# Attention kernel on one Trainium2 core: layer 0 scores in groups of up to seven PSUM banks, and results of three chunks written for the next layer

**The chip, the cores and the metric.** One NeuronCore of one Trainium2 chip. The time is the device time of the kernel in microseconds (us), median of several executions. The executions of one round share a chip; the rounds of the experiments ran on chips 12, 15 and 9, each with the kernel before beside them.

## The reference, cut to what matters

```python
# x: (8, 64, 64, 64) float32, so b=8, c=64, n=4096; c8=8
def layer0(x):                      # 8-channel attention over the pixels
    f = Wf @ x + bf;  g = Wg @ x + bg;  hh = Wh @ x + bh     # (8,n) (8,n) (64,n)
    beta = softmax(einsum('bci,bcj->bij', f, g), axis=2)     # 4096 x 4096 per batch
    return x + einsum('bcj,bij->bci', hh, beta)

def layer1(x):                      # group norm, 64-channel attention, projection
    q, k, v = split(w_qkv @ group_norm(x) + b_qkv)
    attn = softmax(q.T @ k * 64**-0.5)
    return w_proj @ (attn @ v) + b_proj + x

out = layer1(layer0(x))
```

## The kernel before

There are 16 stages: layer 0 of batches 0 and 1, layer 1 of batch 0, then layer 0 and layer 1 in turn, with layer 1 of batch 7 last. A stage has four chunks of 512 queries for each half of the pixels, and each chunk 16 steps over the keys. A layer 0 step makes four score banks (two blocks `p` by two halves `h`), each by one matmul on a 32x128 tile. ScalarE turns them into exponentials, TensorE weighs the values with them on 128x64 tiles, and VectorE adds them up for the softmax's denominator.

The kernel uses eight PSUM banks of 512 columns: three tiles of two banks for scores and products, and two for accumulators.

```python
ps_s = ctx.enter_context(tc.tile_pool(name="ps_s", bufs=3, space=PSUM))   # 3 x 2 banks
ps_a = ctx.enter_context(tc.tile_pool(name="ps_a", bufs=2, space=PSUM))   # 2 x 1 bank
# ...
for i, (at, c) in enumerate(seq):               # every chunk c of every stage
    j = 0
    while j < 2 * NT:                           # 32 blocks of two banks
        due, taken = take(i * NT + (j + at.group) // 2 - 1)   # inserted work of this step
        blocks = range(j, min(j + (2 if taken else at.group), 2 * NT))  # at.group: 3 in layer 0
        group = []
        for j in blocks:                        # scores of this group
            t, p = divmod(j, 2)
            ps = ps_s.tile([P, 2, CW], F32, tag="s", name=...)
            at.scores(ps, t, p, c)
            group.append((j, ps))
        for j, ps in group:                     # one exp of 1024 columns per block
            # ... a new tile e for every second block
            nc.scalar.activation(e[:, p], ps, AF.Exp, scale=at.scale)
        for u in due: u[2]()                    # inserted products, results
        for r in ready: weigh(*r, now)          # weighing of the group BEFORE
        ready = new
```

`take` hands out inserted work that was put down for a step: the projections of the next stage (`fg`, `qk`), its values (`v`), the denominators (`z`), and a chunk's result. Values are a product whose PSUM bank is emptied by a copy on VectorE:

```python
def values(self, src, w, c):
    ps = ps_s.tile([P, 2, CW], F32, tag="s", name=...)
    # ... 32 small matmuls
    self.copy_values(self.vt[...], ps[...])     # copy_values = nc.vector.tensor_copy
```

A finished chunk's result is a chain on VectorE: `reciprocals` (add, reciprocal, then two DMAs that spread it), and `result` (multiply, add to x, statistics of the next layer's norm):

```python
at_step(now + delay, lambda: sums(spare), not spare)
at_step(now + delay + wait, reciprocals, False)
at_step(now + delay + 2 * wait, result, False)
```

## Time and profile before

| | before |
|---|---|
| median time (3 runs) | 3134.6 us |
| TensorE / VectorE / ScalarE busy | 98 / 80 / 66% |
| layer 0 of batches 0 and 1 | 166.8 and 165.2 us |
| layer 0 of batches 2 to 7 | 151.5 us each |
| layer 1 stages | about 233 us each, the last 241 |

A stage here lasts from its first exp to the first exp of the next. The prediction shows the main views. Timelines there have start, duration, engine, line, operation, output <- input, with the idle time before it and its cause in brackets. The columns are engine, what it was to write, what it waited for, then us in total, times, longest.

```profile
PEld s_l L123 <- ACT e_l L659: 54.1, 69, 0.8
...
PE s_l L123 <- ACT e_l L659: 5.2, 13, 0.4
...
PEld s_l L123 <- DVE v_l L282: 2.0, 3, 1.2
...
PE s_l L123 <- DVE v_l L282: 1.1, 2, 0.8
```

Matmuls (the PE rows) wait for exps for 5.2 us, and for value copies (`DVE v_l`) twice, 1.1 us in all. Weight loads wait for copies for 2.0 us; they run ahead of matmuls, so that does not count by itself. The timeline around one such copy (start, duration, engine, line, operation, output <- input, with the idle time before it and its cause in brackets):

```profile
269.18 0.69 PE L123 MATMUL v_l<-wvp,xn_l 64*64 64x64 f32 x32
269.81 1.94 PE L123 MATMUL acc_l<-e_l,v_l 128*64 128x512 f32 x8
...
271.17 0.68 DVE L282 COPY v_l<-v_l 128x512 f32<-128x512 f32 x1
```

The product is over when the next weighing starts, at 269.81, and its copy starts at 271.17, 1.4 us later.

### The profile page before, as it was taken

The numbers are of one execution on the slowest core, as the hardware profiler recorded it, in microseconds if no ns is written. First come the engines' busy times: TensorE is split into PE (matmuls) and PEld (weight loads), VectorE is DVE, ScalarE is ACT, GpSimd is POOL, SyncE is SP. The second block draws the span as 40 slices with busy tenths as digits, with TensorE's granted clock in tenths as the row PEclk, the third lists the DMA queues.
The fourth block names the chain that finished last, engine by engine and source line by source line (L and its number), as shares of the span: only waits on it lengthen the run. The fifth ranks groups of instructions, "written<-read, shape, count | busy, mean of one in ns | idle before, by whom it ended". The sixth has DMA issues, their size and how long they took to land.

```text
span 3133.8 us, 58576 instructions
## 1 busy us (share of the span) xinstructions
PE 3082.4 (98%) x25523; PEld 1145.6 (37%) x25523; DVE 2505.2 (80%) x1624; ACT 2061.3 (66%) x2224; POOL 16.5 (1%) x41
## 2 busy tenths in 40 slices
PE   7999999999999999999999999999999999999998
PEld 2333334433343334433344333343333433333433
DVE  6999777798768987689776897778977699676676
ACT  5787655786557865578655785558855588555554
POOL 2000000000000000000000000000000000000000
PEclk9999999999999999999999999999999999999999
DMA  3000110100101001010010100101001000000000
GB/s 83 21 8 18 25 25 15 31 8 22 25 17 29 8 22 25 18 28 8 22 25 19 28 8 21 30 13 30 10 18 35 8 18 8 5 21 15 12 11 12
DMA packets 61817, 63.15 MB, mean 20 GB/s; under 512 B 34944, under 2 KB 35024, under 8 KB 61552
## 3 DMA queue, kind: packets, MB, share of 16 engines
q1 hardware_dynamic: 60432, 59.16, 7.7%
q8 instruction: 202, 3.31, 0.4%
q14 instruction: 63, 0.52, 0.1%
q0 software_dynamic: 800, 0.15, 0.0%
q10 hardware_dynamic: 320, 0.01, 0.0%
HBM read 25.06 MB, written 8.65 MB: 11 GB/s over the span
## 4 chain that ended last, share of the span: by engine, by line
PE 86%; DVE 6%; ACT 3%; issue 2%; DMA 2%; SPq 1%; ACTq 0%; DVEq 0%
PE acc_l L123 50%; PE s_l L123 32%; DVE esum_l L625 5%; ACT e_l L659 3%; PE z_l L123 1%; PE qk_l L123 1%; PE v_l L123 1%; DMA r_l<-recips 1%; SPq L320 1%; DMA zt_l<-zs_l 0%; PE fg_l L123 0%; DMA recips<-stash 0%; SPq L412 0%; DVE raw_l L344 0%; DMA w<-in_WgT_dram 0%
## 5 line engine op out<-in xcount | busy, mean ns | idle before, releaser
L659 ACT ACTIVATE e_l<-s_l 128x1024 f32<-128x1024 f32 x2048 | 1968.7, 1025 | 1030.9 <-PE s_l L123 1030.6
L625 DVE TENSOR_TENSOR esum_l<-esum_l,e_l 128x2048 f32<-128x2048 f32 x896 | 2050.8, 2289 | 388.6 <-ACT e_l L659 346.8
L123 PE MATMUL acc_l<-e_l,v_l 64*64 64x512 f32 (+1 forms) x8704 | 1106.2, 591 | 0.0
L123 PE MATMUL s_l<-kq_l 64*64 64x512 f32 (+1 forms) x8448 | 1019.5, 586 | 5.7 <-ACT e_l L659 3.3
L123 PE MATMUL acc_l<-e_l,vt_l 128*64 128x512 f32 x3584 | 841.2, 603 | 0.7
L123 PEld LDWEIGHTS acc_l<-e_l,v_l 64*64 64x64 f32 (+1 forms) x8704 | 382.3, 133 | 549.8 <-issue 504.4
L123 PEld LDWEIGHTS s_l<-kq_l 64*64 64x64 f32 (+1 forms) x8448 | 372.0, 134 | 571.3 <-issue 520.3
L123 PEld LDWEIGHTS acc_l<-e_l,vt_l 128*64 128x64 f32 x3584 | 230.5, 137 | 457.7 <-issue 446.8
L123 PE MATMUL s_l<-fg_l 32*128 32x512 f32 x1792 | 230.3, 468 | 14.6 <-ACT e_l L659 8.2
L123 PEld LDWEIGHTS s_l<-fg_l 32*128 32x128 f32 x1792 | 92.2, 183 | 276.4 <-ACT e_l L659 188.5
L625 DVE TENSOR_TENSOR esum_l<-e_l,e_l 128x2048 f32<-128x2048 f32 x64 | 146.2, 2285 | 27.7 <-ACT e_l L659 27.7
L344 DVE TENSOR_TENSOR raw_l<-raw_l,r_l 128x512 f32<-128x512 f32 x64 | 44.1, 689 | 80.0 <-DMA r_l<-recips 79.9
L123 PE MATMUL z_l<-esum_l,ones 128*32 128x512 f32 (+2 forms) x508 | 55.9, 504 | 4.1 <-DVE esum_l L296 2.8
L551 DVE COPY raw_l<-acc_l 128x512 f32<-128x512 f32 x32 | 22.1, 692 | 36.6 <-PE acc_l L123 36.6
L327 DVE RECIPROCAL stash<-zt_l 128x8 f32<-128x8 f32 x63 | 12.7, 202 | 42.4 <-DMA zt_l<-zs_l 41.4
L525 ACT ACTIVATE kq_l<-qk_l,qkb 128x512 f32<-128x512 f32 x64 | 40.7, 696 | 1.3 <-PE qk_l L123 1.3
L296 DVE TENSOR_TENSOR esum_l<-esum_l 128x1024 f32<-128x1024 f32 x32 | 38.9, 1215 | 0.0
L123 PE MATMUL qk_l<-xn_l,wqk 64*64 64x512 f32 x256 | 33.9, 592 | 2.1 <-ACT e_l L659 2.1
L315 ACT COPY zs_l<-z_l 128x512 f32<-128x512 f32 (+1 forms) x63 | 31.1, 494 | 0.2 <-PE z_l L123 0.2
L282 DVE COPY v_l<-v_l 128x512 f32<-128x512 f32 x36 | 24.7, 686 | 6.9 <-PE v_l L123 6.9
L123 PEld LDWEIGHTS v_l<-wh,x 64*64 64x64 f32 x1024 | 22.4, 135 | 15.4 <-issue 13.3
L123 PEld LDWEIGHTS v_l<-wvp,xn_l 64*64 64x64 f32 x1024 | 21.5, 134 | 16.0 <-issue 14.6
(87 smaller groups left out, 360.5 us busy)
## 6 DMA issues: line engine op xcount, KB each, us to landing
r_l<-recips SPq DMA_DIRECT2D x126, 128.0 KB, 2.9
fg_l<-high_l SPq DMA_DIRECT2D x224, 64.0 KB, 2.0
x<-in_x_dram SPq DMA_DIRECT2D x32, 256.0 KB, 4.9
kq_l<-kq_l SPq DMA_DIRECT2D x64, 128.0 KB, 2.3
out_dram<-raw_l SPq DMA_DIRECT2D x64, 128.0 KB, 2.4
kq_l<-high_l SPq DMA_DIRECT2D x32, 64.0 KB, 2.0
zt_l<-zs_l SPq DMA_DIRECT2D x128, 2.0 KB, 1.8
zt_l<-zs_l SPq DMA_DIRECT2D x124, 1.0 KB, 1.7
```

What stands on the lines that cost most here:

```text
L123: in_order(nc.tensor.matmul(*args, **kwargs))
L282: self.copy_values(self.vt[:, :, ts(c, TPC), :], ps[:, :, 0 : TPC * C].rearrange("k p (t c) -> k p t c", c=C),)
L296: nc.vector.tensor_add(esum[:, 0], esum[:, 0], esum[:, 1])
L315: nc.scalar.copy(zs, z[:, 0:width])
L320: nc.sync.dma_start(dst, zs[row : row + 1, :])
L327: nc.vector.reciprocal(rt, zh)
L344: nc.vector.tensor_mul(raw, raw, r)
L525: nc.scalar.activation(self.parts[:, h, cols], ps[:, h, :], AF.Identity, bias=k1["qkb"][:, h : h + 1],)
L551: nc.vector.tensor_copy(raw, acc[0])
L625: nc.vector.tensor_add(esum, first if t == 1 else esum, e)
L659: nc.scalar.activation(e[:, p], ps, AF.Exp, scale=at.scale)
```

## The change

The intent: fewer, larger groups in layer 0, so that TensorE switches between its two tile shapes less often and ScalarE needs fewer instructions; and less VectorE work inside layer 0, by putting results of its first three chunks into layer 1, where VectorE has room.

```diff
-    ps_s = ctx.enter_context(tc.tile_pool(name="ps_s", bufs=3, space=PSUM))
-    ps_a = ctx.enter_context(tc.tile_pool(name="ps_a", bufs=2, space=PSUM))
+    psum = ctx.enter_context(tc.tile_pool(name="psum", bufs=1, space=PSUM))
+    banks = psum.tile([P, 8, CW], F32, name="banks")
+    pairs = [banks[:, 2 * k + 1 : 2 * k + 3, :] for k in range(3)]
+    outer = (0, 7)                      # accumulators; the idle one is the seventh bank
 ...
-            raw = work.tile([P, CW], F32, tag="raw", name=f"raw_{n}")
+            raw = work.tile([P, CW], F32, tag="raw", bufs=4, name=f"raw_{n}")
-            zt = small.tile([P, 2, QP], F32, tag="zt", name=f"zt_{n}")
+            zt = small.tile([P, 2, QP], F32, tag="zt", bufs=5, name=f"zt_{n}")
 ...
-            at = (12, 28) if self.b == 1 else (2, 25)
+            at = (12, 28) if self.b == 1 else (17, 26)
 ...
+        layer1 = (i // NC + 1) * NC * NT
+        if at.kind == 0 and at.b > 0 and c < NC - 1:
+            when = layer1 + 1 + 2 * c
+            steps = (when, when + 3)
+        else:
+            wait = 4 if next_kind == 0 else 3
+            steps = (now + delay + wait, now + delay + 2 * wait)
+        at_step(steps[0], reciprocals, 0)
+        at_step(steps[1], result, 0)
 ...   # layer 0, groups across chunk borders:
+            room = list(range(1, 7))
+            if closed == 0 and taken != BANK:
+                room = sorted(room + [free])
+            if taken == PAIR:
+                lent = 0 if room[-1] == 7 else 2
+                room = [r for r in room if r not in (2 * lent + 1, 2 * lent + 2)]
+            group = list(zip(units[u : u + len(room)], room))
 ...   # exps of up to four banks:
+                first_ = 2 * p + h
+                n_ = min(4 - first_, len(group))
+                nc.scalar.activation(
+                    e.rearrange("k p h n -> k (p h) n")[:, first_ : first_ + n_, :],
+                    banks[:, bank : bank + n_, :], AF.Exp, scale=at.scale,
+                )
```

Cut: other buffer counts, three shifted steps of group norm in batch 0, and layer 1's loop, which keeps its shape.

More of the change, by code (lines that the diff above doesn't have):

```diff
@@ L104, in fast_path, with pair @@
     dram = ctx.enter_context(tc.tile_pool(name="dram", bufs=1, space=bass.MemoryType.DRAM))
-    ps_s = ctx.enter_context(tc.tile_pool(name="ps_s", bufs=3, space=PSUM))
-    ps_a = ctx.enter_context(tc.tile_pool(name="ps_a", bufs=2, space=PSUM))
+    psum = ctx.enter_context(tc.tile_pool(name="psum", bufs=1, space=PSUM))
+    banks = psum.tile([P, 8, CW], F32, name="banks")
+    pairs = [banks[:, 2 * k + 1 : 2 * k + 3, :] for k in range(3)]
+    outer = (0, 7)
+    turn = 0
+    lent = None
+    def pair():
+        nonlocal turn
+        if lent is not None:
+            return pairs[lent]
+        turn += 1
+        return pairs[turn % 3]
     tensor_last = None
@@ L230, in transposed @@
         def transposed():
-            t0 = ps_s.tile([P, 2, CW], F32, tag="s", name="c_ps0")
+            t0 = pair()
             in_order(nc.tensor.transpose(t0[:C, 0, 0:C], wv, ident[0:C, 0:C]))
@@ L236, in product @@
         def product():
-            t1 = ps_s.tile([P, 2, CW], F32, tag="s", name="c_ps1")
+            t1 = pair()
             matmul(
@@ L244, in biases @@
         def biases():
-            t2 = ps_s.tile([P, 2, CW], F32, tag="s", name="c_ps2")
+            t2 = pair()
             for h in range(2):
@@ L272, in values @@
         def values(self, src, w, c):
-            ps = ps_s.tile([P, 2, CW], F32, tag="s", name=f"v_{self.name}_{c}")
+            ps = pair()
             for t in range(TPC):
@@ L296, in finish @@
                     nc.vector.tensor_add(esum[:, 0], esum[:, 0], esum[:, 1])
-            r = work.tile([P, CW], F32, tag="r", name=f"r_{n}")
+            r = None
             def sums(spare):
-                if spare:
-                    z = ps_a.tile([P, CW], F32, tag="a", name=f"z_{n}")
-                else:
-                    z = ps_s.tile([P, 2, CW], F32, tag="s", name=f"z_{n}")[:, 0, :]
-                zs = work.tile([P, CW], F32, tag="zs", name=f"zs_{n}")[:, 0:width]
+                if spare is not None:
+                    z = banks[:, spare, :]
+                else:
+                    z = pair()[:, 0, :]
+                zs = work.tile([P, CW], F32, tag="zs", bufs=1, name=f"zs_{n}")[:, 0:width]
                 for h in range(2):
@@ L320, in sums, with broadcast @@
                         nc.sync.dma_start(dst, zs[row : row + 1, :])
+            def broadcast():
+                nonlocal r
+                r = work.tile([P, CW], F32, tag="r", name=f"r_{n}")
             def reciprocals():
@@ L327, in reciprocals @@
                 nc.vector.reciprocal(rt, zh)
+                broadcast()
                 dealt = recips[index]
@@ L334, in at_once @@
             def at_once():
-                z = ps_s.tile([P, 2, CW], F32, tag="s", name=f"z_{n}")[:, 0, :]
+                broadcast()
+                z = pair()[:, 0, :]
                 for h in range(2):
@@ L355, in fast_path @@
         banks = 1
-        group = 3
         def before(self):
@@ L388, in project @@
             xt = x_tiles[self.b]
-            ps = ps_s.tile([P, 2, CW], F32, tag="s", name=f"fg_{n}")
+            ps = pair()
             for j in range(2):
@@ L415, in project, with scores @@
                             )
-        def scores(self, ps, t, p, c):
-            for h in range(2):
-                rows = ts(2 * h + p, 32)
-                matmul(
-                    ps[:, h, :], self.g[rows, ts(t, P)], self.f[rows, ts(c, CW)],
-                    start=True, stop=True,
-                )
+        def scores(self, ps, t, p, h, c):
+            rows = ts(2 * h + p, 32)
+            matmul(
+                ps, self.g[rows, ts(t, P)], self.f[rows, ts(c, CW)], start=True, stop=True
+            )
         def weigh(self, acc, e, t, p, start, stop):
@@ L443, in fast_path @@
         banks = 2
-        group = 2
         def __init__(self, b, st):
@@ L461, in means @@
             def means():
-                ps = ps_s.tile([P, 2, CW], F32, tag="s", name=f"gm_{n}")
+                ps = pair()
                 matmul(ps[:, 0, 0:1], gavg, mv[:, 0:1], start=True, stop=True)
@@ L470, in deviations @@
             def deviations():
-                ps = ps_s.tile([P, 2, CW], F32, tag="s", name=f"gv_{n}")
+                ps = pair()
                 matmul(ps[:, 0, 0:1], gavg, v, start=True, stop=True)
@@ L491, in normal @@
             def normal(c):
-                xns[c] = work.tile([P, CW], F32, tag="xn", name=f"xn_{n}_{c}")
+                xns[c] = work.tile([P, CW], F32, tag="xn", bufs=1, name=f"xn_{n}_{c}")
                 nc.vector.tensor_scalar(
@@ L500, in begin @@
                 self.project(0, xns[0])
-            at = [16, 20, 24]
+            at = [18, 21, 24] if self.b == 0 else [16, 20, 24]
             units = [(at[0], channels, False), (at[1], means, True), (at[2], deviations, True)]
@@ L513, in project @@
         def project(self, c, xn):
-            ps = ps_s.tile([P, 2, CW], F32, tag="s", name=f"qk_{self.name}_{c}")
+            ps = pair()
             for i in range(2):
@@ L573, in fast_path, with at_step @@
     count = 0
-    def at_step(s, work_, buffer=True):
+    PAIR, BANK = 1, 2
+    def at_step(s, work_, takes=PAIR):
         nonlocal count
-        later.append((s, count, work_, buffer))
+        later.append((s, count, work_, takes))
         later.sort(key=lambda u: u[:2])
@@ L581, in take @@
     def take(s):
-        due, taken = [], False
+        due, taken = [], 0
         for u in [u for u in later if u[0] <= s]:
@@ L614, in weigh @@
         if j == 0:
-            acc = [
-                ps_a.tile([P, CW], F32, tag="a", name=f"acc_{n}_{m}") for m in range(at.banks)
-            ]
+            acc = [banks[:, outer[(c + m) % 2 if at.kind == 0 else m], :] for m in range(at.banks)]
             esum = work.tile([P, 2, 2, CW], F32, tag="esum", name=f"esum_{n}")
@@ L626, in weigh @@
         if t == NT - 1:
-            delay, spare = (5, False) if at.kind == 1 else (7, True)
-            if c == NC - 1:
-                spare = i + 1 < len(seq) and seq[i + 1][0].kind == 0
-            elif at.kind == 1 and c == NC - 2 and i + 2 < len(seq) and seq[i + 2][0].kind == 0:
-                delay = NT
-            works = at.finish(acc, esum, c, i)
-            if len(works) == 1:
-                at_step(now, works[0])
-                return
-            sums, reciprocals, result = works
@@ L637, in weigh @@
-            at_step(now + delay, lambda: sums(spare), not spare)
-            wait = 4 if i + 1 < len(seq) and seq[i + 1][0].kind == 0 else 3
-            at_step(now + delay + wait, reciprocals, False)
-            at_step(now + delay + 2 * wait, result, False)
-    for i, (at, c) in enumerate(seq):
-        j = 0
-        while j < 2 * NT:
-            due, taken = take(i * NT + (j + at.group) // 2 - 1)
-            blocks = range(j, min(j + (2 if taken else at.group), 2 * NT))
-            group = []
-            for j in blocks:
-                t, p = divmod(j, 2)
-                ps = ps_s.tile([P, 2, CW], F32, tag="s", name=f"s_{at.name}_{c}_{j}")
-                at.scores(ps, t, p, c)
-                group.append((j, ps))
-            new = []
-            for j, ps in group:
-                t, p = divmod(j, 2)
-                if p == 0:
-                    e = ppool.tile([P, 2, 2, CW], F32, tag="e", name=f"e_{at.name}_{c}_{t}")
-                nc.scalar.activation(e[:, p], ps, AF.Exp, scale=at.scale)
-                new.append((i, j, e))
-            j = blocks[-1] + 1
-            now = i * NT + j // 2 - 1
-            for u in due:
-                u[2]()
-            for r in ready:
-                weigh(*r, now)
-            ready = new
@@ new lines, in weigh, with finished @@
+            finished(i, now)
+    def finished(i, now):
+        nonlocal closed
+        at, c = seq[i]
+        closed = max(closed, 1)
+        next_kind = seq[i + 1][0].kind if i + 1 < len(seq) else 1
+        works = at.finish(acc, esum, c, i)
+        if len(works) == 1:
+            at_step(now, works[0])
+            return
+        sums, reciprocals, result = works
+        delay = 7 if at.kind == 0 else 5
+        if at.kind == 1 and c == NC - 2 and i + 2 < len(seq) and seq[i + 2][0].kind == 0:
+            delay = NT
+        spare = None
+        if next_kind == 0:
+            spare = outer[c % 2 if at.kind == 0 else 1]
+        if at.kind == 1 and c < NC - 1:
+            spare = None
+        at_step(now + delay, lambda: sums(spare), PAIR if spare is None else BANK)
+        layer1 = (i // NC + 1) * NC * NT
[7 more added lines that the diff above has]
+        at_step(steps[1], result, 0)
@@ new lines, in fast_path, with ended @@
+    closed = 1
+    def ended():
+        nonlocal ready, closed
+        closed = max(closed - 1, 0)
+        for u in due:
+            u[2]()
+            if u[3] == BANK:
+                closed = 1
+        for r in ready:
+            weigh(*r, now)
+        ready = new
+    i = 0
+    while i < len(seq):
+        at, c = seq[i]
+        if at.kind == 1:
+            for j in range(0, 2 * NT, 2):
+                now = i * NT + j // 2
+                due, taken = take(now)
+                t = j // 2
+                new = []
+                both_ps = [pair(), pair()]
+                for p in range(2):
+                    at.scores(both_ps[p], t, p, c)
+                e = ppool.tile([P, 2, 2, CW], F32, tag="e", name=f"e_{at.name}_{c}_{t}")
+                for p in range(2):
+                    nc.scalar.activation(e[:, p], both_ps[p], AF.Exp, scale=at.scale)
+                    new.append((i, j + p, e))
+                ended()
+            i += 1
+            continue
+        last = next(k for k in range(i, len(seq) + 1) if k == len(seq) or seq[k][0].kind == 1)
+        units = [
+            (k, t, p, h)
+            for k in range(i, last) for t in range(NT) for p in range(2) for h in range(2)
+        ]
+        u = 0
+        while u < len(units):
+            k, t = units[u][:2]
+            now = k * NT + t
+            due, taken = take(now + 1)
+            if any(j == 0 for _, j, _ in ready):
+                closed = max(closed, 1)
+            free = outer[1]
+            if ready:
+                free = outer[(ready[-1][0] + 1) % 2]
+                if seq[ready[-1][0]][0].kind == 1:
+                    closed = 1
+            room = list(range(1, 7))
[5 more added lines that the diff above has]
+            group = list(zip(units[u : u + len(room)], room))
+            u += len(group)
+            for (k, t, p, h), bank in group:
+                seq[k][0].scores(banks[:, bank, :], t, p, h, seq[k][1])
+            new = []
+            while group:
+                (k, t, p, h), bank = group[0]
+                first_ = 2 * p + h
+                n_ = min(4 - first_, len(group))
+                at, c = seq[k]
+                if first_ == 0:
+                    e = ppool.tile([P, 2, 2, CW], F32, tag="e", name=f"e_{at.name}_{c}_{t}")
+                nc.scalar.activation(
+                    e.rearrange("k p h n -> k (p h) n")[:, first_ : first_ + n_, :],
+                    banks[:, bank : bank + n_, :], AF.Exp, scale=at.scale,
+                )
+                new += [(k, 2 * t + p, e) for (k, t, p, h), _ in group[:n_] if h == 1]
+                group = group[n_:]
+            ended()
+            lent = None
+        i = last
@@ L668, in fast_path @@
+    now = len(seq) * NT
     for r in ready:
-        weigh(*r, len(seq) * NT)
+        weigh(*r, now)
     bad = const.tile([P, 2], F32, name="bad")
-    bad_ps = ps_a.tile([P, CW], F32, tag="a", name="bad_ps")[0:1, 0:1]
+    bad_ps = banks[0:1, 0, 0:1]
     def bounds(recip, i):
-        ok = work.tile(list(recip.shape), F32, tag="zs", name=f"ok_{i}")
+        ok = work.tile(list(recip.shape), F32, tag="zs", bufs=1, name=f"ok_{i}")
         nc.vector.tensor_scalar(ok, recip, 1.0 / SUM_MAX, None, op0=ALU.is_ge)
```

## The prediction

> **What bounds the kernel now.** I read the page first, then where each layer's exponentials begin in ScalarE's timeline (32 exps of 1024 columns make a chunk, four chunks a stage), then each stage's engines, and last the chain of waits and the timeline inside one stage of layer 0. There are 16 stages: layer 0 of batches 0 and 1 (166.8 and 165.1 us), then layer 1 and layer 0 in turn (about 233 and 151.4 us), with layer 1 of batches 6 and 7 at the end. Busy engines of one stage of layer 0 and the stage of layer 1 after it (columns: stretch, length, busy us of each engine, clock, DMA):
>
> ```profile
> 586.70:738.10 151.40, 150.22 (x824) 46.72 (x820) 143.98 (x83) 125.05 (x136) 0.00 (x0) 1.00 0.08 20
> 738.10:971.00 232.90, 232.68 (x2372) 96.92 (x2368) 168.17 (x120) 132.48 (x143) 0.00 (x0) 1.00 0.08 21
> ```
>
> The columns are TensorE, its weight loads, VectorE, ScalarE. In layer 0 three engines are nearly full (99%, 95%, 83%); layer 1 is TensorE's alone. The change can only earn in layer 0: 1240 of 3134 us. The chain of waits in a layer 0 stage (start, us, what):
>
> ```profile
> 651.39 0.66 PE s_l L123 x5
> 652.05 2.73 PE acc_l L123 x12
> 654.78 0.66 PE s_l L123 x6
> 655.44 2.73 PE acc_l L123 x12
> 658.16 0.43 PE s_l L123 x4
> 658.60 2.73 PE acc_l L123 x12
> 661.32 0.51 PE s_l L123 x4
> 661.83 0.08 ACT e_l L659
> 661.91 0.12 issue
> 662.03 0.04 ACTq L432
> 662.07 0.67 issue
> 662.74 1.94 ACT e_l L659 x2
> 664.68 0.04 issue
> 664.72 0.49 PE s_l L123 x2
> ```
>
> A group is six score matmuls (0.66 us), then the twelve weighing records of the group before (2.73 us; an fp32 matmul leaves two records): 3.39 us, TensorE to TensorE. Only at the chunk's end, where 32 blocks don't divide by three and a group of two follows, does the chain pass to ScalarE: eight weighing records take 1.87 us, the exps of the three blocks before take 2.86, and two scores start about 0.8 us late. ScalarE itself waits in every group, VectorE in none:
>
> ```profile
> 648.48 2.86 ACT L659 ACTIVATE e_l<-s_l 128x1024 f32<-128x1024 f32 x3 [0.53 <-PE s_l L123]
> ...
> 670.83 19.06 DVE L625 TENSOR_TENSOR esum_l<-esum_l,e_l 128x2048 f32<-128x2048 f32 x8
> ```
>
> From 668.44 to 705.85 VectorE has no gap: 37.41 us for a chunk that takes TensorE 37.9. So TensorE sets the end and VectorE is a hair behind it.
>
> **What the Trainium skill says.** (1) "TensorEngine Tiling (Array Packing)", section Tiling Modes, Key Properties: "Changing tiling mode (not just tile) drains the TensorE". The trace agrees. In layer 1 scores and weighing both use 64x64 tiles and sixteen records take 1.72 us; after a z product of another shape they take 1.88:
>
> ```profile
> 764.13 1.00 PE z_l L123 x8
> 765.12 1.88 PE acc_l L123 x16
> 767.00 1.72 PE s_l L123 x16
> 768.72 1.72 PE acc_l L123 x16
> ```
>
> Layer 0 alternates 32x128 scores with 128x64 weighing, so each group pays. (2) "ScalarE: Activation LUTs", section What ACT_TABLE_LOAD costs: 186 ns + 0.833 ns per column, back-to-back overlap of about 93 ns. The trace: 1025 ns for 1024 columns (1039 by the formula), 2.86 us for three in a row, so each further one adds 0.92. Wider exps thus save only about 0.07 to 0.1 us each. (3) "PSUM — Partial Sum Buffer", section PSUM bank collisions: TensorE may not write a bank that ScalarE is reading, so a score waits until the exp that covers its bank is over. An exp over four banks frees them all at its end; no trace of before has one.
>
> **The change part by part.** *TensorE's groups.* I fit a group's time as a fixed part, a round of up to four concurrent scores, and a pair of weighing records. Pair: layer 1's 1.72/4 = 0.43 us per four 64x64 tiles, the same 512 columns, so 0.427. Six scores against four before the same twelve records: 3.39 - 3.16 = 0.23, one round, 0.22. The fixed part is what is left: 3.39 - 0.44 - 6 x 0.427 = 0.38 (drains and weight loads). Six scores are two rounds; so are seven, as their row quarters follow in turn. Seven cost no more than six, apart from their weighing.
>
> Counted in the instruction order, a later layer 0 stage (256 banks) has 44 groups before (40 of six, 4 of four: 84 rounds) and 39 after (24 of seven, 14 of six, 1 of four: 77 rounds). The weighing is 256 pairs x 0.427 = 109.3 us in both. Before: 44 x 0.38 + 84 x 0.22 + 109.3 = 144.5, plus the z products (3 x 0.99 + 2 x 0.57 = 4.1) = 148.6; measured 151.4, so 2.8 us are waits, and the chain shows four of about 0.8. After: 39 x 0.38 + 77 x 0.22 + 109.3 + 4.1 = 145.1. Groups now run across chunks, so the short group that made three of the waits is gone.
>
> *ScalarE.* Estimates from the rows above: 2048 columns take 1.025 + 1024 x 0.836 ns = 1.88 us, seven banks in two or three instructions 3.2 to 3.3. They begin 0.53 after the group's first score and end near 3.8. A group of seven completes three or four pairs of exponentials in turn, so TensorE's period is 3.39 or 4.24 by turns. In the short one the next scores want their last banks at 3.4 to 3.7 and get them at 3.85: 0.1 to 0.3 us lost, in about 12 groups a stage, 2.4 us, and perhaps 0.3 at the edges. So 145.1 + 2.7 = 147.8 us: **3.6 us less in each of six stages, 22 us**.
>
> *The first two stages* (331.9 us). Groups fall from 93 to 83, rounds from 163 to 162: 10 x 0.38 + 0.2 = 4.0 us. By the same sum TensorE has about 290 us of groups and 19 of inserted products, so 23 are waits; about 12 of these are the start until 47 us, which stays. Of the other 11 I take half, since these stages still take a pair of banks for each inserted product and then run groups of four or five. **10 us together.**
>
> *VectorE.* Moving a chunk's result takes away 0.16 + 0.20 + 0.69 + 0.75 + 0.69 = 2.49 us: a chunk falls from 37.41 to 34.9, under TensorE's new 36.9. Without that the wider groups would run into VectorE. In the layer 1 that follows, 3 x 2.49 = 7.5 us land in the first nine steps, where VectorE waits 1.14 us for ScalarE in each step of 3.43: 10.3 us of room. The six exponential buffers allow some 12 us of lag there. So layer 1 pays **nothing**.
>
> Sum: 3134.6 - 22 - 10 = 3102.6; I say **3102 us**, 1.0% faster.
>
> **The rivals.** *The wide exps become the wait.* If banks come free later than I think, all 24 groups of seven lose 0.3 us or more: 7 us a stage, the gain of layer 0 is gone, and the time is 3120 to 3135. For it: an exp holds four banks, and ScalarE's 3.8 is above the short period. Against: over two periods TensorE needs 7.6 and ScalarE 6.6. *VectorE becomes the bound.* Layer 1's last results (raw copies, 1.2 us halving, two results) put it some 6 us behind at a stage's start, and a tile of exponentials that straddles two groups lives longer in its six buffers. ScalarE would then wait for VectorE, a stage would stay at 149 to 150 us, and the time be near 3115. *The waits all go.* Every stage at 145.5 and the first two 17 us shorter gives 3080. *Layer 1 pays:* if the moved results held up TensorE for 2 us in each of seven stages, 14 us of the gain go, 3117. VectorE's idle 1.14 per step speaks against it.
>
> **Range and chances.** The rivals lie between 3080 and 3135, mine in the middle, and three of the four push upwards. I take 3078 to 3122 for 8 in 10. Faster by 2% needs under 3072, more than every wait of layer 0 that I can count: 0.06. Slower by 2% would need a false dependency on the one big tile of banks; the built kernel's waits show scores waiting at the borders of exps alone: 0.02.
>
> **What would show each step.** In the profile after: layer 0 stages of 147 to 148.5 us and layer 1 stages still near 233; periods of about 3.4 and 4.2 by turns with 0.66 before weighing also for seven scores (0.77 would mean that the round is wrong); exps of 2048 columns at 1.88 us; pieces of ScalarE in the chain shorter than 0.3 us and no longer at chunk ends; VectorE with gaps in layer 0; result rows inside the first nine steps of layer 1 with no TensorE wait behind them. The prediction is wrong if the last scores of a group wait longer than 0.3 us, if VectorE stands in layer 0's chain, or if layer 1 grows.

## More of the kernel before

The granted TensorE clock was about 0.995 of full speed in the profiled runs.

TensorE's order is fixed by explicit dependencies. The other engines' order is chosen by the framework's scheduler within the dependencies.

## The result, and the profile after

| | before | after |
|---|---|---|
| median time (4 runs each) | 3134.84 us | 3123.85 us |
| span of the profiled run | 3133.8 us | 3120.9 us |
| first two stages together | 331.9 us | 331.1 us |
| layer 0 of batches 2 to 7, each | 151.5 us | 148.1 us |
| layer 1 of batches 0 to 6, each | 232.2 to 233.2 us | 232.8 to 234.6 us |

The ratio is 0.9965, with a 95% interval of 0.9948 to 0.9983. A ratio here is the mean time of one kernel's fast runs over that of the other's of the same rounds, so it is not quite the ratio of the medians. The gain is 11 us, a third of the 32.6 predicted, and 3123.85 lies just above the predicted range.

The table of stretches for the third layer 0 stage and the layer 1 stage after it (columns as in the prediction):

```profile
587.03:735.12 148.09, 147.39 (x816) 46.71 (x812) 141.60 (x81) 122.69 (x103) 0.00 (x0) 1.00 0.08 21
735.12:969.46 234.34, 234.07 (x2380) 95.86 (x2376) 170.41 (x121) 132.33 (x142) 0.00 (x0) 1.00 0.08 21
```

Layer 0 is 3.4 us shorter. The layer 1 stage seems 1.5 us longer, but that is where the border falls: 16 weighing records of the last layer 0 group now follow layer 1's first scores, instead of 8. That is 3.58 against 1.87 us, 1.7 us carried over the border. A layer 0 stage is therefore best read with the layer 1 stage after it. The six pairs from the start of layer 0 of batch 2 to the start of the last stage took 2305.8 us before and 2293.5 after: **2.05 us less a pair**.

The chain of waits inside that layer 0 stage (start, us, what):

```profile
586.91 2.92 PE banks L137 x27
589.82 0.02 issue
589.85 0.02 ACT e_l L746
589.87 1.75 issue
591.62 1.03 ACT e_l L746
592.65 0.04 issue
592.69 137.98 PE banks L137 x698
```

Where before it passed to ScalarE at the chunks' ends, it now runs 138 us from matmul to matmul. That does not mean without waits: short ones are hidden in its pieces. They show in TensorE's own timeline:

```profile
611.10 0.73 PE L137 MATMUL banks<-fg_l 32*128 32x512 f32 x7
611.76 2.80 PE L137 MATMUL banks<-e_l,vt_l 128*64 128x512 f32 x12
614.49 0.98 PE L137 MATMUL banks<-fg_l 32*128 32x512 f32 x7
615.40 3.65 PE L137 MATMUL banks<-e_l,vt_l 128*64 128x512 f32 x16
```

A run's duration here includes the modelled end of its last matmul, so starts are what to subtract. From 611.10 to 611.76, seven scores take 0.66 us, just as six did before. From 614.49 to 615.40 they take 0.91: after the short weighing (12 records) they wait 0.25 us for the exps. The periods are 3.39 and 4.49 by turns, where 3.39 and 4.24 were the ones without waits.

The exps (line, engine, operation, shapes, count | busy us, mean ns | idle time before and its releaser):

```profile
L746 ACT ACTIVATE e_l<-banks 128x2048 f32<-128x2048 f32 (+3 forms) x757 | 954.9, 1325 | 233.2 <-PE banks L137 226.5
```

757 instructions replace 1024 in layer 0. VectorE's timeline in the middle of the same stage:

```profile
656.72 0.68 DVE L364 TENSOR_TENSOR raw_l<-raw_l,r_l 128x512 f32<-128x512 f32 x1
657.32 2.28 DVE L640 TENSOR_TENSOR esum_l<-esum_l,e_l 128x2048 f32<-128x2048 f32 x1
659.52 0.75 DVE L453 SCALAR_TENSOR_TENSOR x<-raw_l,hb,x 128x512 f32<-128x512 f32 x1
660.30 0.69 DVE L454 BATCH_NORM_STATS2 st_l<-x 128x6 f32<-128x512 f32 x1
```

These are a chunk's result (lines 364, 453 and 454), which the change writes into layer 1 at 735 us. They still run in layer 0. The call was deferred, but the scheduler orders VectorE's instructions, and it put them back where their inputs are ready. **The deferral did not happen.** The built order of the kernel showed this before any run; the prediction overlooked it.

In the first two stages, nothing was gained. Their table of waits (20 to 353 us):

```profile
PEld banks L137 <- DVE v_l L296: 12.4, 5, 4.3
PE banks L137 <- DVE v_l L296: 8.5, 5, 4.0
PE banks L137 <- ACT e_l L746: 5.1, 5, 1.9
```

TensorE now waits 8.5 us for five copies of values, where before it waited 1.1 us for two. The largest of them in the timeline:

```profile
259.97 9.46 DVE L640 TENSOR_TENSOR esum_l<-esum_l,e_l 128x2048 f32<-128x2048 f32 x4
...
262.89 2.80 PE L137 MATMUL banks<-e_l,v_l 128*64 128x512 f32 x12
...
269.35 0.68 DVE L296 COPY v_l<-banks 128x512 f32<-128x512 f32 x1
...
270.09 0.79 PE L137 MATMUL banks<-kq_l 32*128 32x512 f32 x2 [3.97 <-DVE v_l L296]
```

The value product was over at 262.89 us, when the next weighing started. Its copy stands in VectorE's order behind a run of four sums of exponentials and starts at 269.35, 6.5 us later. The scores need its banks (in this stage `f` and `g` lie in a tile called `kq_l`). The clock falls as well; the same stretch by parts:

```profile
265.00:270.00 5.00, 1.12 (x8) 0.19 (x4) 4.90 (x4) 0.60 (x1) 0.00 (x0) 0.84 0.00 0
270.00:275.00 5.00, 4.91 (x14) 1.55 (x16) 2.61 (x3) 2.84 (x3) 0.00 (x0) 0.50 0.00 0
```

The granted clock (third number from the end) is 0.50 in the 5 us after the gap, and one weighing of eight records took 1.74 us too long there. The Trainium skill, "TensorE: Matmul & The Clock Gate", section What's actually happening, says that the array's clock is halved after at least one idle window of some 3.4 us. The idle time here is 3.97 us, but the profile has the clock at 0.50 from 268.44 on, 2.3 us after the idle time began, and other runs had it halved after shorter ones (last section).

To count the waits of a stage I took, in TensorE's timeline, each run of scores less 0.66 us (0.44 for up to four) and each weighing less 0.165 us and 0.2135 us a record. Matmuls slowed by a lower clock count as waits here. The first two stages held 19.9 us of waits before and 23.4 after. So their work fell by 4.4 us (331.9 - 19.9 against 331.1 - 23.4), and waits gave 3.5 of it back. (A count; it is good to about 1 us.)

### The profile page after: what moved, and what is told of

It is laid out like the page before. It is cut to its first block, busy times and chain, and to the rows that moved or that the text cites. A ratio compares the mean times of both kernels' runs of the same rounds, so it can differ in the third digit from the quotient of the medians.

```text
span 3120.9 us, 58240 instructions
## 1 busy us (share of the span) xinstructions
PE 3070.0 (98%) x25523; PEld 1140.2 (37%) x25523; DVE 2504.3 (80%) x1624; ACT 2042.1 (65%) x1957; POOL 16.5 (1%) x41
## 4 chain that ended last, share of the span: by engine, by line
PE 92%; DVE 4%; ACT 2%; issue 1%; DMA 1%; SPq 0%; ACTq 0%; DVEq 0%
PE banks L137 92%; DVE esum_l L640 3%; ACT e_l L746 1%; ACT e_l L705 0%; DMA r_l<-recips 0%; DMA w<-in_WgT_dram 0%; DMA fg_l<-high_l 0%; DVE v_l L296 0%; SPq L334 0%; DVE vt_l L296 0%; DMA zt_l<-zs_l 0%; DVE r_l L359 0%; SPq L431 0%; DMA recips<-stash 0%; DVE high_l L421 0%
## 5 line engine op out<-in xcount | busy, mean ns | idle before, releaser
L705 ACT ACTIVATE e_l<-banks 128x1024 f32<-128x1024 f32 x1024 | 992.9, 1021 | 795.6 <-PE banks L137 763.0
L746 ACT ACTIVATE e_l<-banks 128x2048 f32<-128x2048 f32 (+3 forms) x757 | 954.9, 1325 | 233.2 <-PE banks L137 226.5
L137 PE MATMUL banks<-e_l,v_l 64*64 64x512 f32 (+1 forms) x8704 | 1105.0, 591 | 0.0
L137 PE MATMUL banks<-kq_l 64*64 64x512 f32 (+1 forms) x8448 | 1016.2, 586 | 10.3 <-DVE v_l L296 6.0
L137 PE MATMUL banks<-e_l,vt_l 128*64 128x512 f32 x3584 | 831.6, 601 | 0.7
L137 PEld LDWEIGHTS banks<-e_l,v_l 64*64 64x64 f32 (+1 forms) x8704 | 377.7, 133 | 557.2 <-issue 518.6
L137 PEld LDWEIGHTS banks<-kq_l 64*64 64x64 f32 (+1 forms) x8448 | 367.1, 135 | 576.9 <-issue 522.4
L137 PEld LDWEIGHTS banks<-e_l,vt_l 128*64 128x64 f32 x3584 | 233.0, 136 | 459.0 <-issue 455.3
L137 PE MATMUL banks<-fg_l 32*128 32x512 f32 x1792 | 223.3, 469 | 12.0 <-ACT e_l L746 4.6
L137 PEld LDWEIGHTS banks<-fg_l 32*128 32x128 f32 x1792 | 93.2, 183 | 256.5 <-ACT e_l L746 172.3
```

The lines of the kernel that those rows point to most:

```text
L137: in_order(nc.tensor.matmul(*args, **kwargs))
L705: nc.scalar.activation(e[:, p], both_ps[p], AF.Exp, scale=at.scale)
L746: nc.scalar.activation(e.rearrange("k p h n -> k (p h) n")[:, first_ : first_ + n_, :], banks[:, bank : bank + n_, :], AF.Exp, scale=at.scale,
```

## The experiments

My theory after the first look had two parts. (A) In the later stages the groups save what was predicted, but short waits after seven banks take half of it back, and they come from ScalarE's total time per pair of groups. The rival: an exp of four banks holds its banks too long, and narrower exps would do better. (B) In the first two stages VectorE's late value copies eat the gain, and the deferral is without effect. The rival: VectorE's load is the bound, and a real deferral helps everywhere.

Ten kernels were run; all gave the reference's result. Each ratio is to the kernel before in the same rounds. "Pairs" is the stretch of six pairs defined above.

| run | median us | ratio (95%) | first two | layer 0, later | six pairs |
|---|---|---|---|---|---|
| before | 3134.84 | 1 | 331.9 | 151.5 | 2305.8 |
| after | 3123.85 | 0.9965 (0.9948 to 0.9983) | 331.1 | 148.1 | 2293.5 |
| x1_not_deferred | 3124.28 | 0.9965 (0.9951 to 0.9979) | 331.0 | 148.1 | 2293.2 |
| x2_deferred_for_real | 3122.01 | 0.9959 (0.9945 to 0.9973) | 330.4 | 148.1 | 2293.4 |
| x3_six_banks | 3124.84 | 0.9965 (0.9952 to 0.9979) | 335.3 | 149.0 | 2294.5 |
| x4_exp_1024 | 3125.47 | 0.9970 (0.9957 to 0.9984) | 332.4 | 148.5 | 2295.9 |
| x5_exp_512 | 3140.31 | 1.0015 (1.0000 to 1.0031) | 336.7 | 150.8 | 2309.2 |
| x6_before_deferred | 3134.85 | 1.0002 (0.9988 to 1.0016) | 331.7 | 151.5 | 2305.3 |
| x7_both | 3112.2 | 0.9929 (0.9916 to 0.9943) | 320.6 | 148.1 | 2293.6 |
| x8_values_by_scalar | 3112.62 | 0.9929 (0.9916 to 0.9943) | 320.4 | 148.1 | 2293.7 |
| x9_before_values_by_scalar | 3133.29 | 0.9994 (0.9981 to 1.0008) | 330.5 | 151.5 | 2305.1 |
| x10_scalar_six_banks | 3122.94 | 0.9957 (0.9943 to 0.9970) | 330.0 | 149.0 | 2295.3 |

**x1_not_deferred.** The results stay at their old steps.

```diff
-        if at.kind == 0 and at.b > 0 and c < NC - 1:
+        if False:
```

> The changed kernel with the deferral taken out of its text (results at once, as before), groups and exps as changed. My theory: the scheduler had already put those instructions back at their old places on VectorE, so nothing changes: within 1 us of the changed kernel, 3123 to 3125. Rival, the deferral as written did something (buffers, transfers): 2 us or more away, up if it helped.

Every stage is within 0.3 us of the changed kernel's, the whole the same. The deferral as written did nothing.

**x2_deferred_for_real.** The deferred calls may not be issued before the last sum that VectorE has been given by then.

```diff
-            nc.vector.tensor_add(esum, first if t == 1 else esum, e)
+            vec_last = nc.vector.tensor_add(esum, first if t == 1 else esum, e)
...
+    def behind(work_):
+        def queued():
+            with tc.issue_after(vec_last.ins):
+                work_()
+        return queued
...
+            reciprocals, result = behind(reciprocals), behind(result)
```

> The changed kernel with the deferred results really queued on VectorE behind layer 1's sums (the changed kernel's own instruction order has them still inside layer 0). My theory: in the changed kernel layer 0 of batch 1 (168.2 us) is lengthened by VectorE's backlog, since a value projection's copy sits behind it and TensorE waits 4.0 us for the copy; without 2 x 2.5 us of results ahead of it, that stage falls to 162 to 165 us; the later layer 0 stages (148.1 us, TensorE waiting for ScalarE alone) stay within 0.5 us though VectorE gets gaps there, and layer 1 stays. Time 3118 to 3121. Rival A, the backlog is not what holds TensorE: 3123 to 3125. Rival B, VectorE without gaps is the hidden bound of the later layer 0 stages too: each falls by 1.5 us or more, time 3108 to 3113.

VectorE's timeline at the start of layer 1 shows that it now happens, in gaps that were idle:

```profile
747.42 0.68 DVE L364 TENSOR_TENSOR raw_l<-raw_l,r_l 128x512 f32<-128x512 f32 x1
748.14 0.75 DVE L453 SCALAR_TENSOR_TENSOR x<-raw_l,hb,x 128x512 f32<-128x512 f32 x1
748.92 0.69 DVE L454 BATCH_NORM_STATS2 st_l<-x 128x6 f32<-128x512 f32 x1
```

The second stage fell from 168.2 to 164.8 us, as expected: its matmuls waited 1.4 us less for copies, and the half clock after the longest wait, which had cost 1.7 us, did not come. The later layer 0 stages stayed at 148.1, so VectorE was not their bound, and layer 1 did not grow (234.4 on average in both). The gaps that I expected on VectorE in later layer 0 stages did not come: a chunk took it 35.7 us instead of 37.4, but it worked without a gap as before. What changed is its lag: in the stage shown it ended layer 0's last sum 2.7 us after layer 1's first exp, and 7.6 in the changed kernel. No exp waited for VectorE there in either run, so the lag cost nothing. The whole, 3122.01, lies above the 3118 to 3121 expected and is not told apart from the changed kernel. The first stage, in which nothing is deferred, was 2.8 us longer in the profile. The granted clock was lower there: 0.80 from 26 to 40 us and 0.79 from 78 to 86, against 0.87 and 1.00. At 0.07 of 14 us and 0.21 of 8 us that is 2.7 us. At 79.4 us it fell after an idle time of only 0.79 us. What let it fall in this run is not settled.

**x3_six_banks.** Groups across chunks, but never the seventh bank.

```diff
-            if closed == 0 and taken != BANK:
+            if False:
                 room = sorted(room + [free])
```

> The changed kernel that never takes the seventh bank: 43 groups of six in a later layer 0 stage in place of 39. My theory: groups of seven pay their saving back, as in every second one TensorE waits 0.24 us for the last exp (11 times a stage, 2.6 us). By 0.38 a group and 0.22 a round: 43 x 0.38 + 86 x 0.22 = 35.3 without waits against 39 x 0.38 + 77 x 0.22 + 2.6 = 34.4: a stage goes from 148.1 to 149.0, the whole to 3128 to 3132, and no wait of 0.24 is left in the six-bank groups. Rival, the seventh bank brings its full worth and the waits come from elsewhere: a stage of 151.5, the whole near 3144.

The stage took 149.0 us, as expected, with 43 groups and waits only at its start (0.19 and 0.46 us). The seventh bank's four groups fewer are worth 0.9 us there, but 0.7 of that is the border again: the six pairs differ by 1.0 us, 0.2 each. The whole came out at 3124.84, below the 3128 to 3132 that I expected. I had left out this shift; I had also left out the first two stages, which took 4.2 us more in the profiled run (3127.8 us, the slowest of the five); one exp waited 3.0 us for VectorE's sums there. Groups of six across chunk borders, with the wide exps, bring nearly all of the later stages' gain.

**x4_exp_1024.** The same groups with exps of at most two banks.

```diff
-                n_ = min(4 - first_, len(group))
+                n_ = min(2 - first_ % 2, len(group))
```

> The changed kernel with exps of 1024 columns at most, so four for seven banks in place of two or three. Each further exp costs ScalarE about 0.07 to 0.1 us, so the waits of 0.24 grow to 0.3 to 0.4 us: a later layer 0 stage takes 148.6 to 149.8 us, the whole 3126 to 3134 (3124 in the changed kernel). If width does nothing, 148.1 us and 3124.

The wait after a short weighing rose from 0.25 to 0.31 us, eleven times a stage; a wait of 0.46 us in the last weighing before layer 1 was gone, the only place where I found the wide exp at a disadvantage. The stage rose to 148.5 and the six pairs by 2.4 us, to just under the expectation. On the whole time the intervals of the two ratios overlap, so the 1.6 us between the medians is not told apart. Two runs of TensorE's timeline:

```profile
615.11 1.04 PE L137 MATMUL banks<-fg_l 32*128 32x512 f32 x7
616.07 3.65 PE L137 MATMUL banks<-e_l,vt_l 128*64 128x512 f32 x16
```

**x5_exp_512.** One exp for each bank.

```diff
-                n_ = min(4 - first_, len(group))
+                n_ = 1
```

> The changed kernel with one exp per bank (512 columns), so that each bank is free as soon as its own exp ends, and ScalarE needs about 3.45 to 3.55 us for seven banks in place of 3.25. My theory, the waits of 0.24 come from ScalarE's total time from a group's first score to its last exp: the wait grows to about 0.5 us, a later layer 0 stage to 151 to 152 us, the whole to 3140 to 3150. Rival, the wait comes from one wide exp holding four banks until its end: the waits shrink, a stage takes 147 or less, the whole 3118 or less.

The stage took 150.8 us, just under the 151 to 152 expected, and the whole 3140.31. The wait is now 0.49 us (1.15 between starts, less 0.66):

```profile
616.85 1.22 PE L137 MATMUL banks<-fg_l 32*128 32x512 f32 x7
618.00 3.65 PE L137 MATMUL banks<-e_l,vt_l 128*64 128x512 f32 x16
```

The narrower the exp, the longer the wait after seven banks: 0.25, 0.31, 0.49. The rival, that a wide exp holds its banks too long, would have it the other way round. ScalarE's total time sets these waits. With this, theory A stands.

**x6_before_deferred.** The kernel before with a real deferral (x2's edit), the same buffer counts and the same shifts of inserted work as in the change, and none of the groups.

```diff
+            if at.kind == 0 and at.b > 0 and c < NC - 1:
+                when = (i // NC + 1) * NC * NT + 1 + 2 * c
+                at_step(when, behind(reciprocals), False)
+                at_step(when + 3, behind(result), False)
+                return
```

> The kernel before with its groups of three blocks and exps of 1024 columns, and only the deferral added, really queued behind layer 1's sums. My theory: TensorE, not VectorE, sets the end of layer 0 there, so relief of VectorE alone earns nothing: 3132 to 3136, later layer 0 stages 151.5 within 0.3. Rival, VectorE without gaps at 37.4 us a chunk is half of the bound: a stage falls by 1.5 us or more, the whole under 3126.

No stage moved by more than 0.5 us, and the whole is the same. Room on VectorE by itself earned nothing in the kernel before.

**x8_values_by_scalar.** The changed kernel, with the value copies made in the first two stages (for layer 0 of batch 1 and layer 1 of batch 0) on ScalarE.

```diff
-            self.copy_values(
+            early = self.b == 1 - self.kind
+            (nc.scalar.copy if early else self.copy_values)(
```

> The changed kernel with the eight copies of value projections that fall into the first two layer 0 stages made by ScalarE in place of VectorE, results where the changed kernel has them. In the changed kernel TensorE loses about 10.8 us there behind such copies (1.87 and 1.50 in the first stage, 4.53 + 1.74 + 1.12 in the second, the 1.74 at a lower clock after the long stop). My theory: these copies wait in VectorE's order behind its backlog of sums; ScalarE has none, but the 0.6 us of each copy delays its exps, so 6 to 9 us of the 10.8 come back: the two stages take 322 to 326 us together (331.1 in the changed kernel), the whole 3115 to 3119. Rival, VectorE's sums bound these stages anyway and the stop only moves elsewhere (to the buffers of exponentials): within 2 us of the changed kernel, 3122 to 3126.

3112.62 us, better than expected and 11 us under the changed kernel. The first two stages fell from 331.1 to 320.4. Their table of waits:

```profile
PE banks L137 <- ACT e_l L747: 5.1, 5, 1.9
...
PE banks L137 <- ACT v_l L297: 0.5, 2, 0.3
```

The 8.5 us behind value copies became 0.5, the lower clock after the gap went with it (1.7 us), and the chain of waits from 180 to 360 us is TensorE's again (94.8% of it, against 65.2% and 23.5% of VectorE's sums in the changed kernel). All waits of the two stages are 12.9 us by my count, against 23.4. "Perfetto Trace Analysis", section Optimizing Scalar/DVE Operations, of the Trainium skill says that where VectorE is saturated, moving work to ScalarE may pay; it did here, where VectorE was busy for 299.4 of the 331.1 us, and one copy took 0.59 us on ScalarE against 0.68 on VectorE.

**x7_both.** x8's edit together with x2's.

> The same copies by ScalarE and the deferred results really queued behind layer 1's sums. My theory: once the copies are out of VectorE's order, its backlog no longer holds TensorE, so the deferral adds little: 0 to 2 us under the run with the copies alone, 3114 to 3118. Rival, backlog and copies each hold TensorE by themselves: 3 us or more under it, 3112 or less.

The same as x8 within 0.3 us in every stage; like x8, it came out below the range expected. With the copies out of VectorE's order, the deferral is worth nothing even where it happens. x2's gain in the second stage thus came from the copies, which had fewer instructions ahead of them. Theory B stands, and its rival has fallen.

**x9_before_values_by_scalar.** x8's edit in the kernel before.

> The kernel before with the one edit that took 11 us off the changed kernel: the copies of the value projections made in the first two stages go to ScalarE. Theory: in the kernel before no TensorE wait in these stages hangs on such a copy (its copy came 1.9 us after the product, against 6.4 in the changed kernel), so the edit is worth nothing there: the first two stages stay at 330 to 333 us together and the whole at 3132 to 3136 us. Rival: VectorE's late copies cost 11 us whatever the groups are, and the edit has nothing to do with the change: then some 321 us and 3123 to 3126.

(The 1.9 us in that text count from the product's start, the 6.4 from its end; from the end, they are 1.4 against 6.5. Also, two waits of matmuls did hang on such copies before, 1.1 us in all.)

The first two stages took 1.4 us less together, 3.1 less in the first and 1.7 more in the second, and the clock was at 0.50 at other times than before. On the whole time there is no difference that the interval shows. So x8's 11 us are not a gain that lay there before: the copies only became a large wait when the groups changed.

**x10_scalar_six_banks.** x8's kernel with x3's edit.

> The best kernel so far (values by ScalarE, 3112.6) with groups of at most six banks. Theory: the seventh bank saves 0.4 us a group and the wait after it takes 0.24 back in each short period, so with its last group's bookkeeping it is worth 0.2 us a stage: later layer 0 stages 149.0, layer 1 stages 0.7 us shorter, whole 3112 to 3117 us. Rival: the seventh bank earns its four groups a stage in full (4 x 0.38 us), six stages and two more: some 11 us, 3121 to 3125 us.

The later stages came as expected (149.0), the whole did not: 3122.94 instead of 3112 to 3117. The first two stages took 330.0 us against 320.4 with the seventh bank. I had looked at the later stages alone. In the first two, an inserted product takes a pair of banks and leaves a group of five with the seventh bank, of four without it. By my counts six banks mean 92 groups instead of 83, with 4.2 us more work and 5.4 us more waits. In the later stages the seventh bank is worth some 0.2 us each, and here 9.6 together. Not all of that need be the bank: up to 2.8 us of it was lost at half clock in the first 50 us, which lasted longer in the profile of x10 than in that of x8. In the changed kernel only 4.2 could be seen (x3); matmuls waited 5.3 us for copies there, against 8.5 with the seventh bank. The number fell into the rival's range, but not where the rival had put it.

The version that beats both kernels is thus x8: 0.7% under the kernel before, with x7 no better.

## Why the prediction was wrong

The sum was 22 us in six later stages and 10 in the first two. The profiles show 12.3 and 0.8; the other parts of the program (a start 1.0 us later, the first and last layer 1 stages) cancel within 0.5 us. The profiled spans differ by 12.9 us, the medians by 11.0.

- **TensorE's groups: right.** Seven scores took 0.66 us like six, the weighing 2.73 and 3.58, and the number of groups and rounds was that of the built order.
- **ScalarE: right in kind and size.** A 2048-column exp took 1.88 us, and the waits after short weighings were 11 of about 0.24 us, 2.6 in a stage, where 2.4 was predicted. x4 and x5 confirm their cause.
- **"so 2.8 us are waits" and "perhaps 0.3 at the edges": both too favourable.** The waits of a stage before were 2.1 us: 0.19 and 0.50 at its start and two of 0.71 at chunk ends; the chain was read as "four of about 0.8". The rest of the 2.8 was the error of the fit, which does not go away. After, the edges cost 1.2 us: 0.19 and 0.53 at the start as before, and a new one of 0.46 where layer 1 begins. So waits went from 2.1 to 3.8 instead of from 2.8 to 2.7. Work fell by 3.5, so a pair gains 1.8 by this count, and 2.05 was measured instead of 3.6. This is about 9.7 us of the miss. It rests on counting the waits in the traces; no run tested the edges by themselves.
- **The stage's time met the prediction (148.1 against 147.8), and still the gain was wrong.** The border between the stages moved 1.7 us of layer 0's work behind layer 1's first scores. Checking one side of a border would have called this right.
- **"10 us together": not what happened, at 0.8.** Its two terms were four of groups and half of 11 of waits. With the value copies out of the way (x8) work fell by about 4.5 and waits by 7.0, 11.5 together, up to 2.2 of it because less time fell at half clock. The step failed on what it left out: a copy in VectorE's order behind its backlog of sums, for which matmuls waited 8.5 us instead of 1.1. This is about 9.2 us of the miss.
- **"Moving a chunk's result takes away ... 2.49 us": this is the step that did not happen at all.** The scheduler put the results back. But x2, x6 and x7 show that the later stages would not have been shorter; "Without that the wider groups would run into VectorE" was wrong too. VectorE's 37.4 us a chunk are indeed more than TensorE's 37.0, but the lag reached only 7.6 us at the stage's end, and layer 1 took it up. VectorE was without a gap from 593 us on and yet not on the chain. Where the results really moved, a chunk fell to 35.7 us, not to 34.9.
- **"Layer 1 pays nothing": right for the results**, also where they really move (x2). The stage itself is 1.5 us longer, by the border.
- **The rivals.** VectorE as the bound came true, but in the first two stages and through the order of its work, not in the later ones through its load. The wide exps as a wait were refuted by x5.

Left open: why the scheduler set four sums ahead of the copy at 269 us in the changed kernel and not before, and whether an explicit order on VectorE would do as well as moving the copies.

## What to carry to other kernels

Where a scheduler orders an engine, a call moved in the source has not moved until the built order says so; compare that order before pricing the move. When TensorE gets faster, look for the small copies that give its banks back, and keep them out of the order of an engine that has a backlog. Read a stage together with the one after it, and count its waits one by one instead of taking them as what a fitted sum leaves over.

## What the Trainium skill lacked or had wrong

- "TensorEngine Tiling (Array Packing)", Key Properties, says that a change of tiling mode drains TensorE, but not what it costs. My fit of the kernel before gives 0.38 us for each group's fixed part (two changes and weight loads), and after it the seven-score run of 0.66 us and weighings of 2.73 and 3.58 us agree with the same sum. In layer 1, the weighing after a z product of another shape took 1.88 us instead of 1.72.
- "TensorE: Matmul & The Clock Gate", What's actually happening, puts the halved clock after at least one idle window of some 3.4 us. Here shorter idle times came before it: 2.10 us in x9 (the next weighing of 12 records took 4.02 us instead of 2.73) and 1.60 in x4 (8 records took 3.55 instead of 1.87). An idle time of 2.08 us at the same place in the kernel before left the clock at 1.00.
- "Perfetto Trace Analysis", Optimizing Scalar/DVE Operations, says that where ScalarE is not saturated but causes bubbles on other engines, breaking up its instructions may let work end sooner. Here, with ScalarE busy for 122.7 of 148.1 us, it did the reverse: exps of at most 2048, 1024 and 512 columns left waits of 0.25, 0.31 and 0.49 us on TensorE.
- No page that I found tells that an engine with a gapless timeline need not be the bound, as VectorE here (141.6 of 148.1 us busy, and a real deferral changed nothing), or that it can be one through the order of its instructions alone (8.5 us of waits for five copies of 0.68 us).
